# PSUM laid out anew in a two-layer graph transformer: chains, product tiles, and a standing tile for sums, weights and queries

## The chip, the cores and the metric

The kernel runs on one core of a Trainium2 chip. Its time is device time in microseconds (us) for one launch. The core has five engines that are named here as the profile names them: PE (matrix products; PEld is its loading of weights), DVE (elementwise work and reductions), ACT (activations and copies), POOL (here almost only the issuer of indirect DMAs) and SP (the issuer of plain DMAs). SBUF is the working memory of 128 partitions; PSUM is the smaller memory into which PE writes. PSUM has eight banks, each with 512 f32 per partition.

## The reference

The reference is a heterogeneous graph transformer over 6250 nodes of 128 features and 100000 edges, with 16 node types, 32 edge types, 8 heads of 16 and 2 layers.

```
k, q, v = x @ Wk[type], x @ Wq[type], x @ Wv[type]           # a matrix per node type
kw, m   = (k @ Watt[edge type])[src], (v @ Wmsg[edge type])[src]
a       = (kw * q[dst]).sum(per head) * pri[edge type] / 4
att     = softmax of a over the edges of each dst
hag     = sum over the edges of a dst of m * att
h       = silu(hag @ Wa[type]) * alpha[type] + x * (1 - alpha[type])
x       = layernorm(h) * g + b                               # twice, with weights of its own
out     = layernorm(x0 + x @ ff_w + ff_b)
```

## The kernel before

**Nodes and blocks.** A preparation sorts the nodes by type and degree into 49 blocks of 128. Forty-four blocks hold nodes of one class (four types), 11 blocks for each of four classes; five mixed blocks hold nodes of any of the 16 types. Blocks of one kind are worked on in superblocks of up to four (the mixed ones as 2 and 3).

**Tables.** A table has a row of 256 f32 for each node and edge type: the first half is the key already multiplied by Watt, the second the value multiplied by Wmsg. The table of layer 0 is made before the first edges; the table of layer 1 is made while the edges of layer 0 are worked on. Row groups are products on PE (L354 in `table_block`, a tile `tb` of two banks for each pair of products), copied to SBUF (`st`) by ACT (L362), for the last superblock in turn with DVE (L360), and written out by an indirect DMA on POOL (L1761, 98 of them, two for a block).

**Edges.** `edges(l)` walks the blocks. Each block has slots; a slot is one edge for each of its 128 nodes. For each slot POOL issues one gather (L1528, `kv<-tab,ell`, 819 in a layer) of 128 table rows. Four slots share one of 12 buffers `kv`. DVE multiplies the keys by the query (L1544), sums over each head (L1550), and when the block's slots are there, `finished` makes the softmax: maximum, difference, the exponential on ACT (its result is the weights w), the values times w, their accumulation in `acc`, and a last reduction over the four slots of `acc` into `sums`. One block (`TOP`) has additional slots whose rows are spread over its partitions; its weights stay in SBUF.

**Nodes.** `nodes` finishes a superblock: it normalises, transposes on PE, multiplies by Wa, applies silu and layernorm. In layer 0 it then makes the keys, queries and values of layer 1; in layer 1 the output. A product with a matrix per type is done by masks: for each type DVE writes `xm`, the features with every other type's columns at zero (`masked`), and PE adds up the products over the types in one PSUM tile `nb` (`linear_of`). Queries of the next superblock are made the same way (`queries0`).

**Order.** The steps of these generators are woven into the gather loop: `spread` gives a generator a number of steps over a number of slots, `tick` advances it after each chunk, `step` advances `finished`. The order on PE, DVE and ACT is then settled by a scheduler from the dependencies and the code's order; POOL's and SP's order is that of the code. Many instructions come through one helper and appear in the profile as L267.

**PSUM before**, after the preparation: one bank for `nb`, one bank `hold` for the weights of layer 0, and three tiles `tb` of two banks each, eight banks in all. In layer 0 the query is read from SBUF, where it lies; in layer 1 `query` takes a `tb` tile for each block, into which ACT copies the query (L1353), and the weights and `acc` use the same tile. In layer 0 `acc` is in SBUF.

**Mixed superblocks.** In `linear_of` the transposed features are first copied to SBUF (`h2`) when there are 16 types. For k, q, v of layer 1 the code makes three passes over the types, each with its own 16 masks:

```
for j in range(3):
    outs.append(nps.tile([P, SB * P], F32, name="nb"))
    for t0 in range(0, TY, 2):
        xms = list(masked(npl, types[t0:t0 + 2], ntb, h2, n))
```

Of the kernel before, what the change touches and what calls it, by code (L numbers as in the profile page):

```python
# [10 lines left out]
F32 = mybir.dt.float32  # L11
# [9 lines left out]
P = 128  # L21
# [51 lines left out]
def kernel(  # L73
# [240 lines left out]
    def linear_of(pool, nps, types, ntb, hT, n, w):  # L314
# [888 lines left out]
    def arm(fast):  # L1203
# [99 lines left out]
        def edges(l):  # L1303
# [43 lines left out]
            def query(s, i):  # L1347


                if l == 0:  # L1350
                    return got[s][0][:, i, :], None
                pair = tps.tile([P, 2, SB * P], F32, name="tb")
                nc.scalar.copy(pair[:, 1, :D], got[s][0][:, i, :])  # L1353
                return pair[:, 1, :D], pair

            def moved(pair, by, what, to):
# [8 lines left out]
            def finished(s, i, chunks, kvt, a, pair, sums, den):  # L1365
# [6 lines left out]
                if i0 + i == TOP:  # L1372
                    rest, chunks = kvt[-1], chunks[:-1]
                    moved(pair, node_of, rest[:, 3, :RK * REST * H],
# [13 lines left out]
                if rest is None:  # L1388
                    if l == 0:
                        held = hold_ps.tile([P, SB * P], F32, name="hold")  # L1390
                    w = (pair[:, 1, D:D + K * H] if l else held[:, :K * H]).rearrange(
                        "p (k h) -> p k h", h=H)
                on.scalar.activation(w, av, AF.Exp)
                if rest is not None:
                    moved(pair, rows_of, a[:, OWN:K, :].rearrange("p k h -> p (k h)"),
# [567 lines left out]
```

## Time and profile before

| | us |
|---|---|
| median of 3 runs (lowest to highest) | 3025.17 (3024.95 to 3028.88) |
| profiled execution | 3024.62 |
| its span | 3022.8 |
| preparation and first table | 0 to about 592 |
| gathers of layer 0, and table of layer 1 | about 592 to 1874 |
| gathers of layer 1 and output | about 1874 to 3023 |

The span is the time between the first and the last instruction of the core; the profiled execution's own time is 1.8 us longer. The first gather starts at 591.7 us, the last scatter of the table of layer 1 at 1861.4, and the first gather of layer 1 at 1874.6. Windows of 602 to 1806 and 1874 to 2977 us are used as stretches of layer 0 and layer 1.

In a row of groups, a line, an engine, an operation, and output and inputs by their names in the program are followed by the count, the busy time in us, the mean in ns, and the idle time of that engine just before these instructions with what ended it. In a row of the timeline the first two numbers are start and duration in us; in square brackets stands the idle time before and its releaser. "issue" is time in which an engine waited for nothing that the profile shows.

### The profile page before, as it was taken

How to read it: one execution, taken by the hardware profiler on the slowest of the kernel's cores; microseconds unless marked ns; L12 is line 12 of the kernel's file. 1: busy time of each engine (PE TensorE's matmuls, PEld its weight loads, DVE VectorE, ACT ScalarE, POOL GpSimd, SP SyncE). 2: the span in 40 equal slices, each digit the busy share in tenths (PEclk: the TensorE clock that was granted, in tenths of full speed). 3: DMA queues.
4: the chain of work that ended last, by engine and by line, in shares of the span. 5: the costliest groups of instructions: out<-in, count | busy, mean ns of one | idle time of the engine just before them, and what ended most of it. 6: DMA issues, size and time to landing. Idle time of an engine off the chain costs nothing.

```text
span 3022.8 us, 21562 instructions
## 1 busy us (share of the span) xinstructions
PE 1580.5 (52%) x5325; PEld 703.1 (23%) x5325; DVE 1891.1 (63%) x4383; ACT 978.7 (32%) x1635; POOL 2032.2 (67%) x2116
## 2 busy tenths in 40 slices
PE   5999978413667667777777884021122213221212
PEld 2445434201223322332223332010111001000001
DVE  7467655257657766777666653476576667666665
ACT  3887533200434234434444553011111111111111
POOL 3333665477777777777777762777677777777773
PEclk9999777556777777787777786555555556555555
DMA  7999999943677577867788897333334333333331
GB/s 217 416 418 418 394 392 397 371 107 100 234 275 260 197 248 282 297 225 254 271 303 296 330 354 278 105 110 111 92 103 118 111 111 109 112 109 106 106 100 45
DMA packets 163485, 671.37 MB, mean 222 GB/s; under 512 B 52012, under 2 KB 78926, under 8 KB 138302
## 3 DMA queue, kind: packets, MB, share of 16 engines
q0 software_dynamic: 113152, 635.19, 58.6%
q1 hardware_dynamic: 34218, 27.57, 3.3%
q10 hardware_dynamic: 15976, 7.10, 1.0%
q8 instruction: 46, 0.75, 0.1%
q14 instruction: 93, 0.76, 0.1%
HBM read 245.42 MB, written 425.02 MB: 222 GB/s over the span
## 4 chain that ended last, share of the span: by engine, by line
POOL 24%; issue 17%; DMA 16%; DVE 13%; PE 7%; ACT 3%; ACTq 0%; DVEq 0%; POOLq 0%
POOL kv L1528 21%; DMA kv<-tab,ell 14%; PE nb L267 6%; DVE kv L1544 2%; DVE xm L267 2%; PE tb L354 2%; DVE kv L267 2%; DMA tab<-st,row 2%; DVE a L1550 1%; DVE acc L267 1%; ACT L267 1%; POOL tab L1761 1%; DVE tb L267 1%; DVE hs L267 1%; POOL out_dram L1793 1%
## 5 line engine op out<-in xcount | busy, mean ns | idle before, releaser
L1528 POOL DMA_INDIRECT kv<-tab,ell x1638 | 1615.6, 986 | 542.6 <-issue 437.4
L362 ACT COPY st<-tb 128x512 f32<-128x512 f32 (+1 forms) x984 | 681.6, 777 | 535.4 <-PE tb L354 349.8
L1544 DVE TENSOR_TENSOR kv<-kv,tb 128x512 f32<-128x512 f32 (+3 forms) x223 | 142.7, 640 | 381.1 <-DMA kv<-tab,ell 367.4
L1544 DVE TENSOR_TENSOR kv<-kv,q 128x512 f32<-128x512 f32 (+3 forms) x223 | 142.9, 643 | 324.6 <-DMA kv<-tab,ell 316.1
L354 PE MATMUL tb<-bdv,vT 32*128 32x512 f32 x784 | 266.0, 781 | 45.0 <-ACT st L362 41.5
L1550 DVE TENSOR_REDUCE a<-kv 128x32 f32<-128x512 f32 (+3 forms) x446 | 280.8, 632 | 1.3
L354 PE MATMUL tb<-bdv,kvT 32*128 32x512 f32 x784 | 253.7, 790 | 22.9 <-ACT st L362 22.5
L354 PE MATMUL tb<-bdk,kvT 32*128 32x512 f32 x784 | 257.3, 776 | 7.9 <-ACT st L362 7.3
L267 PE MATMUL nb<-xm,wa 128*128 128x384 f32 (+2 forms) x336 | 178.0, 690 | 148.8 <-DVE xm L267 144.2
L267 PE MATMUL nb<-xm,wkqv 128*128 128x384 f32 (+2 forms) x504 | 218.6, 583 | 48.0 <-DVE xm L267 37.0
L1168 POOL DMA_INDIRECT tab<-st,rows x98 | 101.8, 1039 | 197.7 <-ACT st L362 169.4
L360 DVE COPY st<-tb 128x512 f32<-128x512 f32 (+1 forms) x192 | 128.7, 707 | 145.3 <-PE tb L354 74.7
L267 PE MATMUL nb<-by,all_rows 49*128 49x512 bf16 (+2 forms) x30 | 13.3, 442 | 381.6 <-DVE by L267 353.5
L354 PE MATMUL tb<-bdk,kT 32*128 32x512 f32 x784 | 210.6, 785 | 1.7 <-issue 1.6
L267 PE MATMUL nb<-ident,hag 128*128 128x128 f32 x98 | 24.6, 385 | 284.1 <-DVE hag L267 276.4
L1761 POOL DMA_INDIRECT tab<-st,row x98 | 106.1, 1083 | 80.4 <-DVE st L360 28.0
L267 PEld LDWEIGHTS nb<-xm,wkqv 128*128 128x128 f32 x504 | 106.4, 223 | 174.8 <-issue 88.6
L267 PEld LDWEIGHTS nb<-xm,wa 128*128 128x128 f32 x336 | 85.9, 272 | 240.6 <-issue 184.3
L267 DVE TENSOR_TENSOR tb<-kv,tb 128x512 f32<-128x512 f32 (+3 forms) x216 | 138.2, 640 | 0.2
L267 PE MATMUL nb<-xm,wq 128*128 128x384 f32 (+2 forms) x168 | 92.0, 708 | 87.2 <-DVE xm L267 87.1
L354 PEld LDWEIGHTS tb<-bdv,vT 32*128 32x128 f32 x784 | 98.8, 226 | 147.7 <-ACT st L362 118.9
L1353 ACT COPY tb<-hq 128x128 f32<-128x128 f32 x49 | 13.0, 267 | 369.4 <-DVE sums L267 268.8
(348 smaller groups left out, 2519.9 us busy)
## 6 DMA issues: line engine op xcount, KB each, us to landing
kv<-tab,ell POOLq DMA_INDIRECT x1638
hq<-hqx SPq DMA_DIRECT2D x7, 768.0 KB, 4.8
hqx<-hs SPq DMA_DIRECT2D x7, 512.0 KB, 3.5
hq<-hqx SPq DMA_DIRECT2D x5, 576.0 KB, 4.9
hqx<-xr SPq DMA_DIRECT2D x10, 256.0 KB, 19.2
hqx<-hs SPq DMA_DIRECT2D x5, 384.0 KB, 3.2
hr<-hqx SPq DMA_DIRECT2D x7, 256.0 KB, 5.6
tab<-st,rows POOLq DMA_INDIRECT x98
```

The source lines that it names most:

```text
L267: put = issue(*args, **kwargs)
L354: stream[nc.tensor] = nc.tensor.matmul(pt[:, b], yT[s, i * P:(i + 1) * P], bd[s, tt, :], start=True, stop=True)
L360: nc.vector.tensor_copy(to, pt)
L362: stream[nc.scalar] = nc.scalar.copy(to, pt)
L1168: put = nc.gpsimd.indirect_dma_start(out=tabs[0].rearrange("(n t) c -> n (t c)", t=16), out_offset=bass.IndirectOffsetOnAxis(ap=rows1[:, t ...
L1353: nc.scalar.copy(pair[:, 1, :D], got[s][0][:, i, :])
L1528: get = nc.gpsimd.indirect_dma_start(out=kv[:, j - j0, :], out_offset=None, in_=tabs[l][:], in_offset=bass.IndirectOffsetOnAxis(ap=ell[:, ...
L1544: stream[nc.vector] = nc.vector.tensor_tensor(kk, kk, of.unsqueeze(1).to_broadcast([P, c, D]), op=ALU.mult)
L1550: nc.vector.tensor_reduce(to, kk.rearrange("p k (h d) -> p k h d", h=H), axis=AX.X, op=ALU.add)
L1761: put = nc.gpsimd.indirect_dma_start(out=tabs[1].rearrange("(n t) c -> n (t c)", t=16), out_offset=bass.IndirectOffsetOnAxis(ap=row2[:, tg ...
L1793: put = nc.gpsimd.indirect_dma_start(out=out, out_offset=bass.IndirectOffsetOnAxis(ap=node[:, b:b + 1], axis=0), in_=o[:, i, :], in_offset ...
```

## The change

PSUM after the preparation is divided anew: two banks for `nb`, one standing tile `held` of two banks in place of `hold`, and two tiles `tb` of two banks. Bank 0 of `held` is `acc`, in both layers. The first half of bank 1 holds the weights, and the second half two places for queries that are used in turn. `query` copies the query to one of them by ACT, in layer 0 too. `moved`, which serves the additional slots of `TOP`, takes a `tb` tile in both layers.

For mixed superblocks `linear_of` no longer copies the features to SBUF; its masks read PSUM. k and v are made in one pass over the types with common masks, q in a second. Numbers of steps given to `spread` follow the removed steps.

```diff
@@ linear_of
-        if len(types) > TC:
-            h2 = pool.tile([P, SB * P], F32, name="h2", tag="hb")
-            on.scalar.copy(h2[:, :n], hT[:, :n])
-            yield
-            hT = h2
@@ arm
-        nps = ctx2.enter_context(tc.tile_pool(name="nps", bufs=1 if fast else 5, space=PSUM))
-        hold_ps = ctx2.enter_context(tc.tile_pool(name="hold", bufs=1, space=PSUM)) if fast else None
-        tps = ctx2.enter_context(tc.tile_pool(name="tps", bufs=3, space=PSUM))
+        nps = ctx2.enter_context(tc.tile_pool(name="nps", bufs=2 if fast else 5, space=PSUM))
+        turn, held = [0], None
+        if fast:
+            hold_ps = ctx2.enter_context(tc.tile_pool(name="hold", bufs=1, space=PSUM))
+            held = hold_ps.tile([P, 2, SB * P], F32, name="held")
+        tps = ctx2.enter_context(tc.tile_pool(name="tps", bufs=2 if fast else 3, space=PSUM))
@@ query, moved
-                if l == 0:
-                    return got[s][0][:, i, :], None
-                pair = tps.tile([P, 2, SB * P], F32, name="tb")
-                nc.scalar.copy(pair[:, 1, :D], got[s][0][:, i, :])
-                return pair[:, 1, :D], pair
+                at = (2 + turn[0] % 2) * D
+                turn[0] += 1
+                nc.scalar.copy(held[:, 1, at:at + D], got[s][0][:, i, :])
+                return held[:, 1, at:at + D]
-                ps = pair[:, 1, D:D + n] if pair is not None else tps.tile(
-                    [P, 2, SB * P], F32, name="tb")[:, 0, :n]
+                ps = tps.tile([P, 2, SB * P], F32, name="tb")[:, 0, :n]
@@ finished
-                    if l == 0:
-                        held = hold_ps.tile([P, SB * P], F32, name="hold")
-                    w = (pair[:, 1, D:D + K * H] if l else held[:, :K * H]).rearrange(
-                        "p (k h) -> p k h", h=H)
+                    w = held[:, 1, :K * H].rearrange("p (k h) -> p k h", h=H)
-                if rest is None and l:
-                    acc = pair[:, 0].rearrange("p (k c) -> p k c", k=CH)
-                else:
-                    acc = ep.tile([P, CH, D], F32, name="acc", bufs=1)
+                acc = held[:, 0].rearrange("p (k c) -> p k c", k=CH)
@@ steps of nodes and of queries
-                           (42 if l else 33) + (0 if len(sbs[s][2]) == TC else 14 if l else 58),
+                           (42 if l else 33) + (0 if len(sbs[s][2]) == TC else 13 if l else 41),
-                    spread(work, asked, 25 if mixed(s + 1) else 11 if l == 0 else 8, asking(s))
+                    spread(work, asked, 24 if mixed(s + 1) else 11 if l == 0 else 8, asking(s))
@@ nodes, mixed superblocks of layer 0
-                    for j in range(3):
-                        outs.append(nps.tile([P, SB * P], F32, name="nb"))
+                    for js in ((0, 1), (2,)):
+                        outs += [nps.tile([P, SB * P], F32, name="nb") for _ in js]
                         for t0 in range(0, TY, 2):
                             xms = list(masked(npl, types[t0:t0 + 2], ntb, h2, n))
                             yield
                             for t, xm in xms:
-                                on.tensor.matmul(outs[j][:, :n], wkqv[:, j, t, :], xm[:, :n],
-                                                 start=(t == 0), stop=(t == TY - 1))
+                                for j in js:
+                                    on.tensor.matmul(outs[j][:, :n], wkqv[:, j, t, :], xm[:, :n],
+                                                     start=(t == 0), stop=(t == TY - 1))
```

Over the whole of the program PE has as many instructions as before, DVE 32 fewer, ACT 43 more (49 copies of queries, less 6 of features); POOL and SP have the same instructions in the same order.

How instructions move shows at three places. The first is DVE in layer 0, where the first mixed superblock's masks (`xm`) are woven with the accumulation of the block at hand (`acc`, `hold` before). Before:

```order
L267 SCALAR_TENSOR_TENSOR xm_7726<-ntb_6465,h2_7683 128x256
L267 SCALAR_TENSOR_TENSOR xm_7728<-ntb_6465,h2_7683 128x256
L267 SCALAR_TENSOR_TENSOR xm_7735<-ntb_6465,h2_7683 128x256
L267 SCALAR_TENSOR_TENSOR xm_7737<-ntb_6465,h2_7683 128x256
L267 TENSOR_TENSOR acc_7731<-kv_7541,acc_7731 128x512
L267 SCALAR_TENSOR_TENSOR xm_7748<-ntb_6465,h2_7683 128x256
L267 SCALAR_TENSOR_TENSOR xm_7750<-ntb_6465,h2_7683 128x256
```

After:

```order
L267 SCALAR_TENSOR_TENSOR xm_7713<-ntb_6460,h2_7690 128x256
L267 TENSOR_TENSOR held_5849<-kv_7526,held_5849 128x512
L267 SCALAR_TENSOR_TENSOR xm_7722<-ntb_6460,h2_7690 128x256
L267 TENSOR_TENSOR kv_7589<-kv_7589,held_5849 128x4x128
L267 SCALAR_TENSOR_TENSOR xm_7724<-ntb_6460,h2_7690 128x256
L267 TENSOR_TENSOR held_5849<-kv_7558,held_5849 128x512
L1535 TENSOR_TENSOR kv_7740<-kv_7740,held_5849 128x4x128
```

Masks stand singly between the other instructions now, and the sums, the weights and the query all come from `held_5849`.

The second is ACT at the start of layer 0, where it makes the weights of the first blocks from the scores `a` and the queries of the next superblock. Before:

```order
L267 COPY q<-nb 128x512
L267 ACT_TABLE_LOAD
L267 ACTIVATE hold<-a 128x144
L267 ACTIVATE hold<-a 128x136
L267 ACTIVATE hold<-a 128x128
L267 CAST ntb<-nb 128x384
L267 ACTIVATE hold<-a 128x120
```

After:

```order
L267 COPY q<-nb 128x512
L267 ACT_TABLE_LOAD
L267 ACTIVATE held<-a 128x144
L1351 COPY held<-q 128x128
L267 ACTIVATE held<-a 128x136
L1351 COPY held<-q 128x128
L267 ACTIVATE held<-a 128x128
L1351 COPY held<-q 128x128
```

A copy of a query stands between each two exponentials. It writes the tile that the previous block's reduction into `sums` still reads, and waits for that reduction.

The third is PE at the joint of the layers, where the last superblock's k (`kvT0`), v (`kvT1`) and q of layer 1 and the last table products are made. Before:

```order
L267 MATMUL nb_12594<-xm_12585,wkqv_91 128x256
L354 MATMUL tb_12614<-bdk_94,kvT0_12592 128x512
L267 MATMUL nb_12601<-xm_12579,wkqv_91 128x256
L267 MATMUL nb_12601<-xm_12581,wkqv_91 128x256
L267 MATMUL nb_12601<-xm_12583,wkqv_91 128x256
L267 MATMUL nb_12601<-xm_12585,wkqv_91 128x256
L354 MATMUL tb_12614<-bdk_94,kvT0_12592 128x512
L267 MATMUL nb_12608<-ident_69,qT_12606 128x128 x2
```

After:

```order
L267 MATMUL nb_12475<-xm_12466,wkqv_91 128x256
L267 MATMUL nb_12482<-xm_12460,wkqv_91 128x256
L267 MATMUL nb_12482<-xm_12462,wkqv_91 128x256
L267 MATMUL nb_12482<-xm_12464,wkqv_91 128x256
L267 MATMUL nb_12482<-xm_12466,wkqv_91 128x256
L349 MATMUL tb_12495<-bdk_94,kvT0_12473 128x512
L267 MATMUL nb_12489<-ident_69,qT_12487 128x128 x2
L349 MATMUL tb_12495<-bdk_94,kvT0_12473 128x512
```

The first table product (L354 before, L349 now) no longer stands between v and q; both of its halves come after the products for q.

More of the change, by code (lines that the diff above doesn't have):

```diff
@@ L1373, in finished @@
                     rest, chunks = kvt[-1], chunks[:-1]
-                    moved(pair, node_of, rest[:, 3, :RK * REST * H],
+                    moved(node_of, rest[:, 3, :RK * REST * H],
                           a[:, OWN:K, :].rearrange("p k h -> p (k h)"))
@@ L1442, in finished @@
                                             op=ALU.add)
-                    moved(pair, node_of, rest[:, 2, D:], rest[:, 2, :D])
+                    moved(node_of, rest[:, 2, D:], rest[:, 2, :D])
                     yield
@@ L1492, in edges @@
             before = iter(())
-            q, pair = query(0, 0)
+            q = query(0, 0)
             for s, (i0, k, types) in enumerate(sbs):
@@ L1541, in edges @@
                         if rest:
-                            moved(pair, rows_of, got[s][0][:, i, :], kv[:, 2, :D])
+                            moved(rows_of, got[s][0][:, i, :], kv[:, 2, :D])
                         of = kv[:, 2, :D] if rest else q
@@ L1566, in edges @@
                         step(end=True)
-                    before = finished(s, i, chunks, kvt, a, pair, sums, den)
-                    q, pair = then[0] if then else (None, None)
+                    before = finished(s, i, chunks, kvt, a, sums, den)
+                    q = then[0] if then else None
             for _ in before:
```

9 lines of the change are left out of this document (5 added, 4 removed).

## The prediction

> **What bounds the kernel now.** I read the page first, then the chain of waits, then the span cut at the two layers.
>
> ```profile
> span 3022.8 us, 21562 instructions
> PE 1580.5 (52%) x5325; PEld 703.1 (23%) x5325; DVE 1891.1 (63%) x4383; ACT 978.7 (32%) x1635; POOL 2032.2 (67%) x2116
> ...
> POOL 24%; issue 17%; DMA 16%; DVE 13%; PE 7%; ACT 3%; ACTq 0%; DVEq 0%; POOLq 0%
> ...
> L1528 POOL DMA_INDIRECT kv<-tab,ell x1638 | 1615.6, 986 | 542.6 <-issue 437.4
> ```
>
> No engine is busy throughout, but the gathers of L1528 are half of the span alone, and POOL with the issue time before its instructions leads the chain. The windows by layer (columns: stretch, length, then busy time of PE, PEld, DVE, ACT, POOL, then the granted clock, DMA share, GB/s) and POOL's waits of layer 0 (total, times, longest) say how far that goes:
>
> ```profile
> 602.00:1806.00 1204.00, 832.30 (x2572) 339.52 (x2572) 799.08 (x1749) 471.52 (x639) 923.47 (x902) 0.74 0.71 251
> 1874.00:2977.00 1103.00, 210.75 (x463) 106.29 (x463) 694.10 (x1693) 146.53 (x302) 827.93 (x864) 0.54 0.37 108
> ```
> ```profile
> POOL kv L1528 <- issue: 214.2, 703, 0.3
> ...
> POOL tab L1761 <- ACT st L362: 15.1, 14, 3.5
> POOL kv L1528 <- DMA kv<-tab,ell: 11.2, 33, 1.2
> ```
>
> In layer 0 POOL is busy 923.5 us, and each of its 902 instructions has about 0.3 us of issue ahead of it (214.2/703): 923.5 + 902 x 0.305 = 1198 of 1204 us. POOL is full there. What shortens or lengthens a gather of layer 0 moves the end by that much; DVE has 1204 - 799 = 405 us to spare, ACT 732. Layer 1 adds up the same way (827.9 + 864 x 0.305 = 1091 of 1103).
>
> The same windows for the gathers alone (POOL busy and count):
>
> ```profile
> 602.00:1806.00 1204.00, 825.36 (x812) 0.74 0.71 251
> 1250.00:1430.00 180.00, 125.71 (x116) 0.79 0.69 247
> 1600.00:1800.00 200.00, 129.35 (x133) 0.74 0.88 324
> 1874.00:2977.00 1103.00, 782.08 (x819) 0.54 0.37 108
> ```
>
> The instruction is one and the same, yet takes 1016.5 ns in layer 0 (825.36/812) and 954.9 ns in layer 1 (782.08/819). It is not the DMA traffic: at 324 GB/s a gather takes 972.6 ns, at 247 GB/s 1083.7. The timeline in the first mixed superblock shows what is beside a long one:
>
> ```profile
> 1008.64 0.74 DVE L267 SCALAR_TENSOR_TENSOR xm<-ntb,h 128x256 f32<-128x256 bf16 x2
> 1008.87 2.81 POOL L1528 DMA_INDIRECT kv<-tab,ell  x1 [0.30 <-DVE sums L267]
> ...
> 1009.31 0.68 DVE L1544 TENSOR_TENSOR kv<-kv,q 128x512 f32<-128x512 f32 x1
> 1009.91 0.28 DVE L267 TENSOR_TENSOR a<-a,neg 128x128 f32<-128x128 f32 x1
> ...
> 1010.11 0.74 DVE L267 SCALAR_TENSOR_TENSOR xm<-ntb,h 128x256 f32<-128x256 bf16 x2
> ...
> 1032.09 0.95 POOL L1528 DMA_INDIRECT kv<-tab,ell  x1 [0.30 <-issue]
> 1033.34 0.95 POOL L1528 DMA_INDIRECT kv<-tab,ell  x1 [0.30 <-issue]
> ```
>
> The gather of 2.81 us runs under a train of DVE instructions that read two operands from SBUF; the two of 0.95 us run while DVE is idle. What separates the layers is just this: layer 1 keeps q, weights and sums in PSUM, layer 0 only the weights.
>
> [...]
>
> **The change, part by part.** The DVE groups of layer 0 (busy, mean ns | idle before), and the two of layer 1 that show the PSUM forms:
>
> ```profile
> L1544 DVE TENSOR_TENSOR kv<-kv,q 128x512 f32<-128x512 f32 x184 | 126.8, 689 | 298.4 <-DMA kv<-tab,ell 290.0 <-ACT q L267 7.6 <-issue 0.6
> L267 DVE TENSOR_TENSOR acc<-kv,acc 128x512 f32<-128x512 f32 x131 | 89.5, 683 | 0.0
> L267 DVE TENSOR_REDUCE sums<-acc 128x128 f32<-128x512 f32 x48 | 50.0, 1041 | 0.1
> L267 DVE SCALAR_TENSOR_TENSOR xm<-ntb,h 128x384 f32<-128x384 bf16 x80 | 41.1, 551 | 8.6 <-PE nb L267 4.0 <-ACT h L267 3.8
> L267 DVE SCALAR_TENSOR_TENSOR xm<-ntb,h 128x256 f32<-128x256 bf16 x80 | 30.1, 414 | 5.6 <-PE nb L267 5.4 <-ACT h L267 0.2
> L267 DVE SCALAR_TENSOR_TENSOR xm<-ntb,nb 128x384 f32<-128x384 bf16 x48 | 23.3, 546 | 2.5 <-PE nb L267 2.5
> ```
> ```profile
> L1544 DVE TENSOR_TENSOR kv<-kv,tb 128x512 f32<-128x512 f32 x183 | 125.5, 686 | 358.8 <-DMA kv<-tab,ell 345.1 <-issue 13.4
> L267 DVE TENSOR_REDUCE sums<-tb 128x128 f32<-128x512 f32 x46 | 31.2, 678 | 0.0
> ```
>
> 1. *Gathers.* q and the sums of layer 0 go to PSUM: kv<-kv,q and acc<-kv,acc lose their second SBUF operand. Of the 160 masks xm<-ntb,h, 96 are for k, q, v: 32 vanish, 64 stay in SBUF; the other 64 (Wq and Wa) now read PSUM. Busy time with two SBUF operands: 126.8 + 89.5 + 41.1 + 30.1 = 287.5 us before, (64/160) x 71.2 = 28.5 after, so 90% goes. The excess of layer 0's gathers is 812 x (1016.5 - 954.9) ns = 50.0 us; 90% is 45. Since the longest gather stands in a burst of masks, what stays may weigh more than its time, so I take **-42**. Bounds: -50 (all of it) and 0 (the cause is another).
>
> 2. *Scatters* share POOL and its fate (columns of the second: min, median, max ns):
>
> ```profile
> 602.00:1806.00 1204.00, 98.11 (x90) 0.74 0.71 251
> ```
> ```profile
> L1761 POOL DMA_INDIRECT tab<-st,row x98: 973/1013/3374, 779.2 to 1861.4; - x98
> ```
>
> 98.11 - 90 x 1.013 = 6.9 us over the median: **-5**, bounds -7 and 0.
>
> 3. *DVE itself.* PSUM operands are no dearer: 689 and 686 ns for the multiplication, 546 for a mask from PSUM against 551. The reduction of sums drops from 1041 to about 678 ns (48 x 0.36 = 17 us), the 32 masks are some 15 us. DVE's slack of 405 us hides all of this: 0 in the sum. If DVE had no slack it would be -32.
>
> [...]
>
> 4. *Query copies.* Layer 0 gets 49 copies of q on ACT. Layer 1 had them:
>
> ```profile
> L1353 ACT COPY tb<-hq 128x128 f32<-128x128 f32 x49 | 13.0, 267 | 369.4 <-DVE sums L267 268.8
> ```
>
> The copy must wait for the previous block's sums, since query and sums share one tile; behind it on ACT's queue stand product copies and the next exponentials, and the next block's multiplication, then its kv buffers, then POOL wait for it. In layer 1 that multiplication names no ACT wait at all, only 13.4 us of issue. In layer 0 ACT also copies products (1.01 us each, below). Bounds: 0, and 48 x (0.27 + half of 1.01) = 37 us if nothing is absorbed. Twelve kv buffers hold 48 gathers, near 60 us of POOL's time, so a lateness of 0.8 us mostly vanishes; I take **+3**, near the lower end.
>
> 5. *Two product tiles for three.* In mid-layer ACT empties them:
>
> ```profile
> PE tb L354 <- ACT st L362: 26.9, 34, 5.4
> ```
> ```profile
> ACT st L362 <- PE tb L354: 269.4, 120, 22.1
> ```
>
> ACT waits for products ten times as long as PE waits for a free tile: PE is late here, not the tiles. Nothing mid-layer; bounds 0 and the price in rival two. The joint between the layers is another matter, there nothing gathers:
>
> ```profile
> 1841.41 1.12 PE L354 MATMUL tb<-bdk,kvT 32*128 32x512 f32 x2
> ...
> 1847.01 2.36 DVE L360 COPY st<-tb 128x1024 f32<-128x1024 f32 x2 [12.41 <-PE tb L354]
> ...
> 1853.03 1.19 PE L354 MATMUL tb<-bdv,kvT 32*128 32x512 f32 x8 [0.25 <-DVE st L360]
> ...
> 1854.20 1.01 ACT L362 COPY st<-tb 128x1024 f32<-128x1024 f32 x1 [1.17 <-PE tb L354]
> ...
> 1859.43 1.23 DVE L360 COPY st<-tb 128x1024 f32<-128x1024 f32 x1 [0.99 <-PE tb L354]
> ...
> 1861.41 0.97 POOL L1761 DMA_INDIRECT tab<-st,row  x1 [4.17 <-issue]
> ...
> 1874.62 0.99 POOL L1528 DMA_INDIRECT kv<-tab,ell  x1 [12.24 <-DMA tab<-st,row]
> ```
>
> The last superblock's 16 products are emptied from 1847.01 to 1860.66, 13.65 us, by ACT and DVE in turn. With two tiles a pair is filled (1.19) and then emptied (1.23): 1.23 + 7 x 2.42 = 18.2, or +4.5. Against it, k, v and q follow on PE without a table matmul of 1.12 us between them and with a bank more for chains, about -1.4; the sums are 0.36 shorter twice, -0.7; leftover products of the superblock before now compete for two tiles, about +1.5. I take **+4**, bounds 0 and +10.
>
> 6. *Layer 1* already had this layout; its sums move to another tile: 0.
>
> Sum: -42 - 5 + 3 + 4 = -40. The profiled execution is 3024.62 us, 1.8 of it around the span; 3024.62 - 40 = 2984.6. The median of the runs is 0.55 above the profiled one, so **2985 us**.
>
> **The rivals.**
>
> *The gathers stay long.* If what lengthens them is something else that layer 0 does (products, scatters), terms 1 and 2 are gone and 3 and 4 stay: 3024.6 + 7 + 0.55 = 3032. For it: the cause is read from neighbours in time alone. Against it: the pair of rows at 1008.87 and 1032.09.
>
> *Two product tiles become the bound of layer 0.* This is the case on the other side. The scatters stand in POOL's order between the gathers; a late product stops the gathers behind it, which the 15.1 us of tab<-ACT st already show. 98 scatters take four tiles each (two for keys, two for values), 196 pairs; if each pair lost half a fill, 0.3 us (from 1.19/2 for one tile), that is 59 us: 3025.2 - 47 + 7 + 59 = 3044. It decides from 40 us on, that is 0.41 us per scatter. For it: the clock there is 0.74 and PE the busiest engine after POOL (832 of 1204). Against: ACT's 269.4 us of waiting for products.
>
> *The query copies come late.* Half of term 4's upper bound or more reaches POOL: 3025.2 - 47 + 4 + (18 to 37) = 3000 to 3019, the middle 3010.
>
> *All of it comes.* -50 and -7 in full, joint and copies at 0, and DVE being lighter ends some of the small waits: 2957 to 2967.
>
> **How the numbers follow.** Main case 0.68, query copies 0.10, all of it 0.12, gathers stay 0.05, two tiles bind 0.05. A measurement of this kernel can tell about 0.2%, 6 us, from no change: faster is below 3019, slower above 3031. Faster: 0.68 + 0.12 + nearly all of 0.10 = 0.89. Same: 0.01 of the late copies and 0.03 of the first rival, 0.04. Slower: 0.05 + 0.02 = 0.07. The main case alone spans about 2972 to 2998 (joint and copies at their ends, gathers at -50 to -35). The range, 2962 to 3014, takes in most of the copies' case and half of the full gain and leaves out about 0.17.
>
> **What would show it.** Right: a mean of the gathers of layer 0 of 0.965 us or less (1.0165 now), with the stretch from the first gather to the last scatter some 45 us shorter; POOL still full there; DVE's masks from nb 64 more. The joint from the last product's matmul to the first gather of layer 1 some 4 us longer. Layer 1 unchanged within 5 us. Wrong: gathers still over 1.0 us (the cause), tab<-ACT st over 40 us (the tiles), or an idle of POOL put down to kv buffers with ACT held<-q before it (the copies).

## The result and the profile after

The changed kernel takes 2977.36 us (median of 4 runs, 2976.48 to 2982.34), the kernel before 3025.06 us beside it (3022.4 to 3028.88): ratio 0.9842, 95% interval 0.9828 to 0.9855. Forecast were 2985 us, 2962 to 3014.

The page of the changed kernel:

```profile
span 2976.3 us, 21675 instructions
PE 1670.6 (56%) x5325; PEld 727.2 (24%) x5325; DVE 1895.5 (64%) x4351; ACT 996.6 (33%) x1678; POOL 1975.7 (66%) x2116
...
L1519 POOL DMA_INDIRECT kv<-tab,ell x1638 | 1566.8, 957 | 531.6 <-issue 422.5
```

The gathers (L1519 now) are 48.8 us shorter in all. The windows of the gathers' line, of layer 0 and of layer 1 (stretch, length, POOL's busy time and count, granted clock, DMA share, GB/s), before:

```profile
591.00:1802.00 1211.00, 833.48 (x819) 0.74 0.71 250
1874.00:2977.00 1103.00, 782.08 (x819) 0.54 0.37 108
```

and after:

```profile
593.00:1760.00 1167.00, 786.56 (x819) 0.71 0.74 260
1844.00:2935.00 1091.00, 780.27 (x819) 0.54 0.37 109
```

Layer 0's gathers fell from 1.0177 to 0.9604 us each while more DMA traffic ran beside them (260 GB/s, 250 before). To see where the rest of the time went, the span is cut at the first and last gather of each layer. POOL's timeline at the joint of the layers, before (the rest of it stands in the prediction):

```profile
1801.03 0.97 POOL L1528 DMA_INDIRECT kv<-tab,ell  x1 [0.31 <-DVE acc L267]
...
1822.68 0.97 POOL L1761 DMA_INDIRECT tab<-st,row  x1 [4.68 <-ACT st L362]
1850.11 0.97 POOL L1761 DMA_INDIRECT tab<-st,row  x1 [26.46 <-DVE st L360]
```

and after:

```profile
1758.09 0.98 POOL L1519 DMA_INDIRECT kv<-tab,ell  x1 [0.30 <-DVE held L267]
1764.54 1.01 POOL L1753 DMA_INDIRECT tab<-st,row  x1 [5.47 <-ACT qT L267]
...
1788.63 0.97 POOL L1753 DMA_INDIRECT tab<-st,row  x1 [5.45 <-ACT st L357]
1814.95 0.97 POOL L1753 DMA_INDIRECT tab<-st,row  x1 [25.35 <-DVE st L355]
...
1835.53 0.97 POOL L1753 DMA_INDIRECT tab<-st,row  x1 [5.89 <-issue]
1844.87 0.99 POOL L1519 DMA_INDIRECT kv<-tab,ell  x1 [8.37 <-DMA tab<-st,row]
```

| stretch, us | before | after | difference |
|---|---|---|---|
| to the first gather | 591.7 | 593.8 | +2.0 |
| layer 0, first to last gather | 1210.3 | 1165.3 | -44.9 |
| joint, to the first gather of layer 1 | 72.6 | 85.8 | +13.2 |
| layer 1, first to last gather | 1101.8 | 1090.0 | -11.8 |
| after the last gather | 46.4 | 41.5 | -4.9 |
| span | 3022.8 | 2976.3 | -46.5 |

So layer 0 gave what was forecast, the joint lost three times as much, and layer 1 with what follows its last gather, forecast at nothing, gave 16.7 us. The layer 0 row is made of -46.9 us of gathers, -5.7 us of scatters and +7.6 us of gaps between POOL's instructions.

The +13.2 us of the joint have four parts. Nine scatters stand there in both kernels, five with products left over from the superblock before the last and four of the last one. From the last gather to the fifth scatter it took 30.5 us, 21.6 before (+8.9); from there to the first of the last four 26.3, 27.4 before (-1.1); the last four span 20.6, 11.3 before (+9.3); and from the last scatter to the first gather of layer 1 it took 9.3, 13.2 before (-3.9).

In the last four scatters' stretch ACT and DVE copy the products in turn. Four rows of that after:

```profile
1815.78 1.01 ACT L357 COPY st<-tb 128x1024 f32<-128x1024 f32 x1 [2.20 <-PE tb L349]
1816.40 1.23 DVE L355 COPY st<-tb 128x1024 f32<-128x1024 f32 x1 [2.20 <-PE tb L349]
...
1818.97 1.01 ACT L357 COPY st<-tb 128x1024 f32<-128x1024 f32 x1 [2.17 <-PE tb L349]
1819.83 1.23 DVE L355 COPY st<-tb 128x1024 f32<-128x1024 f32 x1 [2.20 <-PE tb L349]
```

Each copy is as long as before (1.01 and 1.23 us), but each waits 2.2 us for its tile to be filled; a pair takes 3.43 us, not 2.4. PE's granted clock in that stretch (length, PE's busy time, clock) was 1.00 before and 0.51 after:

```profile
1845.00:1859.00 14.00, 11.70 (x64) 1.00 0.58 243
```
```profile
1810.00:1834.00 24.00, 21.91 (x57) 0.51 0.60 250
1836.00:1846.00 10.00, 0.00 (x0) 0.50 0.96 370
```

Layer 1: the 11 us are one stall, at the block with additional slots (`TOP`). Its 28 slots hold eight of the twelve buffers until its softmax is done. Before, DVE began that softmax (`a<-a,neg` of 336 columns) when 227 gathers of layer 1 were out and the buffers full, and POOL waited:

```profile
2173.59 0.50 DVE L267 TENSOR_TENSOR a<-a,neg 128x336 f32<-128x336 f32 x1
...
2181.30 1.22 POOL L1528 DMA_INDIRECT kv<-tab,ell  x1 [11.29 <-DVE t L267]
```

After, DVE began it when 222 were out; it stood earlier in DVE's order, behind 58 of layer 1's multiplications with the query and not behind 61, ahead of some that wait for later gathers:

```profile
2134.09 0.50 DVE L267 TENSOR_TENSOR a<-a,neg 128x336 f32<-128x336 f32 x1
...
2142.19 0.94 POOL L1519 DMA_INDIRECT kv<-tab,ell  x1 [1.52 <-DVE held L267]
```

### The profile page after: what moved, and what is told of

It reads as the page before. It is cut to its first block, busy times and chain, and to the rows that moved or that the text cites. A ratio compares the mean times of both kernels' runs of the same rounds, so it can differ in the third digit from the quotient of the medians.

```text
span 2976.3 us, 21675 instructions
## 1 busy us (share of the span) xinstructions
PE 1670.6 (56%) x5325; PEld 727.2 (24%) x5325; DVE 1895.5 (64%) x4351; ACT 996.6 (33%) x1678; POOL 1975.7 (66%) x2116
## 5 line engine op out<-in xcount | busy, mean ns | idle before, releaser
L1519 POOL DMA_INDIRECT kv<-tab,ell x1638 | 1566.8, 957 | 531.6 <-issue 422.5
L1535 DVE TENSOR_TENSOR kv<-kv,held 128x512 f32<-128x512 f32 (+3 forms) x446 | 284.9, 640 | 549.7 <-DMA kv<-tab,ell 459.5
L349 PE MATMUL tb<-bdk,kvT 32*128 32x512 f32 x784 | 295.9, 888 | 45.9 <-ACT st L357 45.7
L349 PE MATMUL tb<-bdv,kvT 32*128 32x512 f32 x784 | 286.3, 898 | 42.0 <-ACT st L357 41.6
L267 DVE TENSOR_TENSOR held<-kv,held 128x512 f32<-128x512 f32 (+3 forms) x444 | 287.2, 647 | 8.7
L349 PE MATMUL tb<-bdv,vT 32*128 32x512 f32 x784 | 261.8, 789 | 50.6 <-ACT st L357 46.5
L267 PE MATMUL nb<-xm,wa 128*128 128x384 f32 (+2 forms) x336 | 185.7, 716 | 88.7 <-DVE xm L267 84.8
L267 PE MATMUL nb<-xm,wkqv 128*128 128x384 f32 (+2 forms) x504 | 205.5, 562 | 10.2 <-DVE xm L267 10.2
L267 DVE TENSOR_TENSOR kv<-kv,held 128x512 f32<-128x512 f32 (+3 forms) x336 | 208.9, 622 | 2.2
L349 PE MATMUL tb<-bdk,kT 32*128 32x512 f32 x784 | 207.6, 790 | 2.4 <-issue 1.6
L267 DVE SCALAR_TENSOR_TENSOR xm<-ntb,nb 128x512 f32<-128x512 bf16 (+2 forms) x304 | 157.3, 562 | 32.3 <-PE nb L267 30.1
L1753 POOL DMA_INDIRECT tab<-st,row x98 | 100.0, 1020 | 103.2 <-DVE st L355 37.1
L267 ACT ACTIVATE held<-a 128x128 f32<-128x128 f32 (+7 forms) x96 | 27.5, 287 | 325.9 <-DVE a L267 182.4
L267 PEld LDWEIGHTS nb<-xm,wkqv 128*128 128x128 f32 x504 | 104.5, 216 | 121.7 <-issue 46.9
L349 PEld LDWEIGHTS tb<-bdv,vT 32*128 32x128 f32 x784 | 97.1, 228 | 148.4 <-ACT st L357 118.4
```

The source lines that it names most:

```text
L267: put = issue(*args, **kwargs)
L349: stream[nc.tensor] = nc.tensor.matmul(pt[:, b], yT[s, i * P:(i + 1) * P], bd[s, tt, :], start=True, stop=True)
L1519: get = nc.gpsimd.indirect_dma_start(out=kv[:, j - j0, :], out_offset=None, in_=tabs[l][:], in_offset=bass.IndirectOffsetOnAxis(ap=ell[:, ...
L1535: stream[nc.vector] = nc.vector.tensor_tensor(kk, kk, of.unsqueeze(1).to_broadcast([P, c, D]), op=ALU.mult)
L1753: put = nc.gpsimd.indirect_dma_start(out=tabs[1].rearrange("(n t) c -> n (t c)", t=16), out_offset=bass.IndirectOffsetOnAxis(ap=row2[:, tg ...
```

## The experiments

Each run's profile was cut into the same stretches. "Changed" is the changed kernel; times are medians, with the ratio to the kernel before and its 95% interval; a profile shows one execution. How far executions differ by themselves can be read from kernels in which a layer is written alike. The gathers of layer 0 add up to 786.5 to 788.2 us in the five kernels that have the changed layer 0, those of layer 1 to 780.3 to 783.5 us in the seven that have the changed layer 1. The gaps between POOL's instructions in layer 0 come to 283.9 to 291.9 us in the former, and their layer 0 to 1162.2 to 1169.0 us.

**Does a second SBUF operand lengthen the gathers?** Three runs each put one operand of the changed kernel back into SBUF.

```diff
# the query of layer 0 (of layer 1 in the third run)
+                if l == 0:
+                    return got[s][0][:, i, :]
                 at = (2 + turn[0] % 2) * D
# acc of layer 0
+                if l == 0:
+                    acc = ep.tile([P, CH, D], F32, name="acc", bufs=1)
```

> The changed kernel, but layer 0 reads its query from SBUF again, without the 49 copies; all else stays. Theory (a DVE instruction with two SBUF operands lengthens the gather beside it): the 143 us of kv<-kv,q in layer 0 have two SBUF operands again. Before, 320 us of such instructions went with 50 us of excess, 0.156 us per us: the gathers of layer 0 grow by 22 us, their mean from 0.960 to about 0.987 us, and the time from 2977 to 2992 to 3002 us. Rival A (only the masks lengthen gathers): mean stays at 0.960, time 2975 to 2980. Rival B (the query copies cost time): the time falls below 2975.

Measured 2999.08 us (0.9908, 0.9891 to 0.9924). Layer 0 is 25.2 us longer, of which gathers 16.7 us and scatters 2:

```profile
593.00:1785.00 1192.00, 803.31 (x819) 0.70 0.73 255
```

> The changed kernel, but acc of layer 0 is a tile in SBUF again; all else stays. Theory of the two SBUF operands: 106 us of acc<-kv,acc at 0.156 us per us make 16 us, the mean of the gathers of layer 0 goes from 0.960 to about 0.980 us, the time to 2988 to 2998 us. Rival A (only the masks): 2977 to 2980 us, the mean stays.

Measured 2988.32 us (0.987, 0.9853 to 0.9886), at the lower end of the expected range: the median is 11 us above the changed kernel's, the profiled execution 16. Gathers were 19.1 us longer:

```profile
595.00:1779.00 1184.00, 805.68 (x819) 0.71 0.73 256
```

> The changed kernel, but layer 1, where no table is made and PE and ACT are nearly idle, reads its query from SBUF; layer 0 stays as changed. The original kernel had the query of layer 1 in PSUM too, so this makes the contention anew where it never was. Theory of the two SBUF operands: about 141 us of the multiplication in layer 1 at 0.156 make 22 us; the mean of the gathers of layer 1 goes from 0.953 to about 0.98 us and the time to 2992 to 3002 us; layer 0 stays at 0.960. Rival C (the long gathers belong to the work on tables in layer 0, its products and scatters): layer 1 stays at 0.953 and the time at 2977.

Measured 3001.74 us (0.992, 0.9903 to 0.9936), in the expected range but for another reason. Layer 1's gathers grew by 7.0 us only, and layer 0's stayed:

```profile
591.00:1759.00 1168.00, 787.18 (x819) 0.70 0.74 260
1844.00:2953.00 1109.00, 787.35 (x819) 0.54 0.37 107
```

The rest is the stall at `TOP`, back with 11.7 us, and the end after the last gather, back at 47.3 us. So the query and the sums carry 36 of layer 0's 47 us, but the price of 0.156 us per us of DVE work did not hold: 0.117 for the query and 0.18 for the sums in layer 0, and 0.05 at most in layer 1, where 3 of the 7 us are within what executions differ by.

That three effects of like size stood in one total called for a run that changes the memory and leaves the waits alone.

```diff
-            held = hold_ps.tile([P, 2, SB * P], F32, name="held")
+            held = npl.tile([P, SB * P + 200 + D], F32, name="held")
-                at = (2 + turn[0] % 2) * D
+                at = SB * P + 200
-            ntb = npl.tile([P, SB * P], BF16, name="ntb", bufs=4)
+            ntb = npl.tile([P, SB * P], BF16, name="ntb", bufs=3)
```

> The changed kernel with the standing tile in SBUF in place of PSUM: sums, weights and query stay one tile, written and waited for by the same instructions, but all its readers on DVE have two SBUF operands. For its room the query has one place, not two, and the types of a superblock have three buffers, not four. Measured so far: undoing the query alone in layer 0 added 16.7 us to the gathers (0.117 us per us of such DVE work), the sums alone 19.1 us, the query alone in layer 1 only 7.0 us (0.05). Theory (the place in memory lengthens the gathers): in layer 0 query, weights and sums together are about 380 us of DVE work, so gathers grow by 44 to 69 us, to a mean of 1.015 to 1.045 us; in layer 1 by 20 to 45 us, to 0.977 to 1.007 us. The stall of 11 us at the block with additional slots and the end after the last gather (46 or 41 us): if the wait of the query's copy for the whole standing tile is what put these right in the changed kernel, they stay away here, since the waits are the same; time 3041 to 3091 us. If the place in memory did it, they come back, 16 us more. Rival (only the order of instructions changed the gathers): means stay near 0.960 and 0.953, time 2977 to 2985 us.

With one place for the query, the last multiplications of a block read the query of the next block, so the scores are computed with a wrong query in part; the instructions and their shapes are the same. Measured 3119.29 us (1.0317, 1.0299 to 1.0334):

```profile
590.00:1819.00 1229.00, 852.41 (x819) 0.72 0.70 247
1899.00:3066.00 1167.00, 849.17 (x819) 0.54 0.35 102
```

Gathers are 65.8 us longer in layer 0 (within the expected 44 to 69) and 68.9 us longer in layer 1 (expected 20 to 45). Layer 1 has no table work, moves 102 GB/s and its PE is busy for 213 of 1167 us, and yet its gathers take 1.037 us as layer 0's take 1.041: products, scatters and traffic of layer 0 are not the cause. The memory of DVE's operands is. The stall at `TOP` was 6.4 us, between the two expectations; the end stayed at 40.4 us.

**The masks.** Two runs: the last masks with two SBUF operands moved to PSUM, and the whole part on mixed superblocks undone (one bank for chains, features copied to SBUF, three passes).

```diff
# masks of k, q, v from PSUM
-                    h2 = npl.tile([P, SB * P], F32, name="h2", tag="hb")
-                    on.scalar.copy(h2[:, :n], hT[:, :n])
+                    h2 = hT
-                    for js in ((0, 1), (2,)):
+                    for js in ((0,), (1,), (2,)):
```

> The changed kernel, but the masks for k, q, v of mixed superblocks read the features from PSUM, as those for Wa do, in three passes (32 masks more, one copy per superblock less). Theory: the last 28.5 us of masks with two SBUF operands go; at 0.117 to 0.156 us per us that is 3 to 4.5 us, more if masks weigh more, as the prediction held: mean of the gathers of layer 0 from 0.960 to 0.953 to 0.956 us, time 2970 to 2974 us. Rival: the 32 masks more and the bank held over all passes make nodes late in mixed superblocks; an idle of POOL appears and the time is above 2980 us.

Measured 2979.44 us (0.9851, 0.9835 to 0.9868). The gathers took 0.9567 us each, 3.1 us less in all, near what was expected; the time did not move (layer 0 was 1165.1 us long, as in the changed kernel). Layers 0 that are written alike differ by 7 us from one execution to another, so 3 us cannot be found again there.

```diff
# part on mixed superblocks undone
-bufs=2 if fast else 5, space=PSUM
+bufs=1 if fast else 5, space=PSUM
+        if len(types) > TC:
+            h2 = pool.tile([P, SB * P], F32, name="h2", tag="hb")
+            on.scalar.copy(h2[:, :n], hT[:, :n])
-                    for js in ((0, 1), (2,)):
+                    for js in ((0,), (1,), (2,)):
```

> The changed kernel without its part on mixed superblocks and chains: one bank for chains, features copied to SBUF in front of the masks, three passes for k, q, v. Standing tile and two product tiles stay (one bank idle). By the prediction's terms: 43 us of masks with two SBUF operands are back, 5 to 7 us of gathers, and at the joint k, q, v wait for their copies again, 1.4 us: 2983 to 2987 us. Rival (the second bank for chains is what made layer 1 and the end of the kernel shorter, as its nodes ran in chains there): layer 1's stall and the end come back with 16 us, 2995 to 3003 us.

Measured 3003.14 us (0.9934, 0.9917 to 0.995), 26 us above the changed kernel, its profiled execution 17 us above. The time is at the upper edge of the rival's range, but not for the rival's reason: the stall did not come back and the end was 43.1 us. The gathers of layer 0 took 5.0 us more, as the masks' 43 us should, and its scatters and gaps 6 more; the joint was 2 us longer, layer 1 and the end 4 and 1.6. The 4 us of layer 1 are gathers, not gaps (784.7 us against 780.3; its 32 masks for mixed superblocks read SBUF again, and part of it may be chance). The other 9 us of the median this one trace does not show. So the second bank may be worth more than its masks, but no single wait was found for it.

**What ended the stall in layer 1?** First suspect was the small products for `TOP`, which shared a tile with the query.

```diff
-                ps = pair[:, 1, D:D + n] if pair is not None else tps.tile(
-                    [P, 2, SB * P], F32, name="tb")[:, 0, :n]
+                ps = tps.tile([P, 2, SB * P], F32, name="tb")[:, 0, :n]
```

> The original kernel, but the three small products for the block with additional slots take a product tile of their own in layer 1 too, as in the changed kernel. Theory M (they waited on the tile that they shared with the query): the stall of 11.3 us in layer 1 goes, time 3013 to 3017 us. Theory W (the stall is a matter of the order on DVE, which the query copy's wait in the changed kernel shifts): the stall stays, 10 to 12 us, and the time is 3021 to 3029 us.

Measured 3026.65 us (1.0003, 0.9993 to 1.0013), the stall 11.4 us: it was not the products' tile. Next, the query's copy out of the standing tile, in the kernel with one bank for chains, which leaves a bank free:

```diff
+            own_q = hold_ps.tile([P, SB * P], F32, name="own_q")
-                nc.scalar.copy(held[:, 1, at:at + D], got[s][0][:, i, :])
-                return held[:, 1, at:at + D]
+                nc.scalar.copy(own_q[:, at:at + D], got[s][0][:, i, :])
+                return own_q[:, at:at + D]
```

> The kernel without the part on mixed superblocks and chains (3003 us), and the query copies go to a bank of their own, so that they wait for no reduction any more; memory of all operands stays PSUM. Theory W: without that wait the stall of 10 to 12 us in layer 1 comes back, and 3 to 5 us at the end; in layer 0 POOL's gaps grow by about 6 us, as they did when the copies were left out; gathers keep their mean of 0.967 and 0.958. Time 3017 to 3026 us. Rival (the place in memory or the number of tiles did it): 3000 to 3006 us.

Measured 3020.46 us (0.9987, 0.9977 to 0.9997), against 3003.14 with the query in the standing tile. All operands are in PSUM as before, and POOL's timeline has the stall again; the end is 47.0 us, 4 us longer:

```profile
2166.40 1.21 POOL L1525 DMA_INDIRECT kv<-tab,ell  x1 [11.35 <-DVE t L267]
```

In all kernels here in which sums, weights and layer 1's query share one standing tile in PSUM, the stall is away; in the two in which that query lies elsewhere (in SBUF, in a bank of its own) it is back with 11.7 and 11.4 us. What changed is the order in which DVE is given its work. In every trace without the stall the softmax of `TOP` comes behind 58 of layer 1's multiplications, with 222 gathers out; in every trace with 11 us of stall behind 61, with 227 out; with the standing tile in SBUF, 6.4 us, behind 60, with 226 out. The last pair of kernels differs in the query's tile alone, so the query's place in the standing tile set this order. That it did so because the copy has to wait for the readers of that tile is argued, not shown: the scheduler goes by dependencies, and these are what the place changes. Which of those readers would matter is open, as the next run shows.

**Two product tiles.** The change of three tiles to two alone, on the original kernel:

```diff
-        tps = ctx2.enter_context(tc.tile_pool(name="tps", bufs=3, space=PSUM))
+        tps = ctx2.enter_context(tc.tile_pool(name="tps", bufs=2 if fast else 3, space=PSUM))
```

> The original kernel with two product tiles in place of three and nothing else changed. In layer 1, where the query, the weights and the sums of a block take one of these tiles, the copy of the next query must now wait for the block before it, as in the changed kernel. Theory: layer 0 between the gathers keeps its length within 5 us (rival two of the prediction: 40 to 59 us longer); the joint grows by 10 to 14 us, with the granted clock near 0.51 in its last stretch; and by theory W (the query copy's wait changes the order on DVE) the stall of 11 us in layer 1 and 5 us of the end go. Time 3018 to 3026 us. Without theory W: 3033 to 3041 us.

Measured 3049.16 us (1.0073, 1.0057 to 1.009), 24 us slower and above both expected ranges. Layer 0 grew by 6.7 us, not 40 to 59; the joint by 14.5; layer 1 by 3.6, and the stall stayed (11.3 us), so a wait for the block before alone does not move DVE's order. This refutes that form of theory W: the copy in the changed kernel also waits for the multiplications of the block at hand, which read the same tile, and that may be what matters.

At the joint the standing tile is idle. It can be the third product tile for the last superblock:

```diff
+        class Three:
+            def tile(self, *args, **kwargs):
+                third[0] += 1
+                return held if third[0] % 3 == 0 else tps.tile(*args, **kwargs)
-                yield from steps(table_block(ep, tps, kT, vT, i, share, STB, store,
+                yield from steps(table_block(ep, Three() if share else tps, kT, vT, i, share, STB, store,
```

> The changed kernel, but the products of the last superblock take the standing tile, idle at the joint, as a third product tile in turn. Theory (at the joint filling and emptying take turns since there are two tiles): a pair took 2.2 us of filling plus 1.23 us of emptying, 3.43 us; with three tiles it takes what PE needs, 2.2 to 2.4 us, so eight pairs end 7 to 9 us earlier and the time is 2968 to 2971 us. Rival D (PE at its granted clock of 0.50 is the limit): less than 2 us, 2975 to 2979 us.

Measured 2968.9 us (0.9803, 0.9781 to 0.9824), the lowest median here and in the range of the theory. But its four runs lie in two groups, at 2963 to 2964 and at 2974 to 2975 us, and the median falls between them; the profiled execution is one of the longer. In it the last four scatters span 11.3 us, not 20.6, as in the kernel before; the way from the last scatter to the first gather is 3.6 us longer again, so the joint is 6.5 us shorter. The clock is 1.00 again:

```profile
1811.00:1826.00 15.00, 12.21 (x63) 1.00 0.63 262
```

Is the low clock the cause or a companion? A run kept PE busy with two tiles:

```diff
+                    for _ in range(2 if warm is not None else 0):
+                        stream[nc.tensor] = nc.tensor.matmul(
+                            warm[:, :2 * P], ident, kT[:, :2 * P], start=True, stop=True)
```

> The changed kernel with its two product tiles, but at the joint PE makes two further products of 128x256 after each tile, into a bank that nothing reads; the wanted work is the same. With two tiles PE's granted clock in the last stretch of the joint was 0.51 in each of the kernels run so far, with three tiles 1.00. Theory K (waiting between fills lets the clock drop, and the low clock doubles the fills): with PE kept busy the clock is above 0.8 there, a pair takes 1.14 + 1.23 = 2.4 us as the prediction had it, the last four scatters span 12 to 15 us in place of 20.6, and the time is 2967 to 2973 us. Rival (the clock is low there for another reason): the further products of 0.93 us per tile come on top of fills at 0.51, four scatters span over 22 us, time 2979 to 2987 us.

Measured 2983.71 us (0.9863, 0.9845 to 0.9881). The clock rose to 1.00, as theory K said:

```profile
1806.00:1834.00 28.00, 28.00 (x108) 1.00 0.55 214
```

But the time went up. The further products took 1.06 us per tile, not half of that as I had reckoned, so PE, busy for all of the 28 us, spent 2.12 us on each tile and was itself the limit (four scatters in 25.4 us). What the run shows is that a tile was filled in 1.06 us at a clock of 1.00, where the changed kernel takes 2.2, and that with the further products PE was granted 1.00 in this stretch, 0.51 without them. What two tiles would take there at the full clock, 1.06 + 1.23 = 2.3 us a pair, was not seen.

Two tiles at the full clock can be seen earlier in the joint, where ACT alone empties the products left over from the superblock before. The changed kernel, and the kernel whose query has a bank of its own:

```profile
1770.00:1789.00 19.00, 18.49 (x48) 0.50 0.85 359
```
```profile
1782.00:1800.00 18.00, 16.14 (x63) 1.00 0.93 391
```

Scatters are 6.4 us apart in the first and 4.5 us in the second. A scatter needs four tiles, so two fills and two copies one after the other: 2 x (2.2 + 1.01) = 6.4 us, or, with the fill of 1.13 us that the second trace shows, 2 x (1.13 + 1.01) = 4.3 us. Both kernels have two tiles, so two tiles do not by themselves bring the low clock. What brought it in one and not in the other is open.

One more attempt let DVE help with the superblock before the last as well:

```diff
-                table(pieces_of(i0, k, outs[0], outs[1], (2,) if final else ()))
+                table(pieces_of(i0, k, outs[0], outs[1], (2,) if fast and i0 in (sbs[-1][0], sbs[-2][0]) else ()))
```

> The kernel with the standing tile as third product tile at the joint (2969 us), and DVE also copies half of the products of the superblock before the last, whose last five scatters come after the last gather of layer 0, 5.4 us apart. Theory (ACT alone empties them there): they come 3.5 to 4.5 us apart, time 2960 to 2966 us. Rival (DVE's copies delay the last block's softmax, or PE at its clock of 0.6 is what is late): 2966 to 2973 us.

Measured 2976.75 us (0.9837, 0.982 to 0.9853), 8 us above the median without it and above both expected ranges: the five scatters came 6.8 to 7.1 us from start to start, 6.1 to 6.4 without it (the 5.4 us of the expectation is the idle time between them). The clock there was 0.67 (0.63 without it), and ACT's copies had not been what was late. The fills at the low clock are the larger part of each turn, and a turn with DVE's copy is longer, 2.2 + 1.23 = 3.43 us against 2.2 + 1.01; two turns make a scatter's 6.9 us.

## Why the prediction was right, and where it was not

**Term 1, the gathers (-42 forecast): right.** -46.9 us. Taking the parts back one by one gave 16.7 (query), 19.1 (sums) and 5.0 us (masks and chains), 41 of the 47; the other 6 no run took back. The bursts of masks, which the prediction held to weigh more, show no sign of it: 3.1 us for the last 28.5 us of them, 5.0 for 43, 0.11 to 0.12 us per us, each figure known to some 2 us.

**Term 2, the scatters (-5): right.** In layer 0 their mean fell from 98.11/90 = 1.090 us to 1.024:

```profile
604.00:1756.00 1152.00, 90.11 (x88) 0.71 0.74 260
```

**Term 3, DVE (0): right.** The groups of layer 0 after show no dearer operand in PSUM (684 against 689 ns, 692 against 683), and sums at 686 ns against 1041:

```profile
L1535 DVE TENSOR_TENSOR kv<-kv,held 128x512 f32<-128x512 f32 x181 | 123.8, 684 | 188.9 <-DMA kv<-tab,ell 133.2 <-ACT held L1351 51.9 <-ACT st L357 2.2
...
L267 DVE TENSOR_TENSOR held<-kv,held 128x512 f32<-128x512 f32 x172 | 119.1, 692 | 3.3
...
L267 DVE TENSOR_REDUCE sums<-held 128x128 f32<-128x512 f32 x47 | 32.2, 686 | 0.7
```

**Term 4, the query copies (+3): the mechanism was mis-seen.** The first row above shows that the copies did come late: the multiplication waited 51.9 us for them, more than the upper bound of 37. The wait for data of gathers fell from 290.0 to 133.2 us at the same time, so it was mostly time in which DVE would have waited anyway. And leaving the copies out did not shorten layer 0's gaps (293.7 us, 287.6 with them, 6 us that are not clear of the 8 by which executions differ). The buffers absorbed the late copies, as far as POOL goes, and the rival fell with that. The 7.6 us of gaps belong for the larger part to the next term.

**Term 5, two tiles.** Nothing mid-layer: nearly right. PE waits for tiles three times as long (26.9 us before):

```profile
PE tb L349 <- ACT st L357: 83.0, 90, 7.7
```

The rival on the other side needed this lateness at the scatters. Most of it stayed on PE, but not all. POOL's waits for product copies between the first and the last gather of layer 0 (total, times, longest), before and after:

```profile
POOL tab L1761 <- ACT st L362: 5.4, 11, 2.1
```
```profile
POOL tab L1753 <- ACT st L357: 9.8, 13, 5.5
```

With two tiles alone they came to 16.4 us, and layer 0 grew by 6.7 us, far from the 40 that the rival needed.

The joint, +4 forecast with bounds 0 and +10, came to +13.2. The step that failed is the fill of 1.19 us, taken from rows at a clock of 1.00 and used for a stretch that was then granted 0.51. The serial form, fill and then empty, was right: 2.2 + 1.23 = 3.43 us a pair, and the last four scatters cost +9.3 us where +4.5 was reckoned. The second term that was too small is that of the leftover products, put at about +1.5: they cost +8.9. Of these, +5.2 lie between the five scatters and have the same reason, since fill and copy by ACT take turns there as well, at a clock of 0.50 (24.0 us against 18.9 before, and 18.6 with two tiles at the full clock); +3.7 are a later first scatter. Against these stand -1.1 in place of -2.1 for k, v, q and the sums, and -3.9 that the sum did not have: the first gather of layer 1 came sooner behind the last scatter (12.24 us of waiting before, 8.37 after, 11.94 with the third tile). Why, no run shows.

**Term 6, layer 1 (0): wrong by 16.7 us.** The argument was that layer 1 had the layout already. It had the memory (but for 32 masks of 15 us in all), not the order: with the query in the standing tile DVE gets another order, and the stall of 11 us, which the profile of before showed, goes. With it go some 5 us at the end, for which the runs show no cause of its own; the end was 46 to 47 us in every kernel with the stall of 11 us and 40 to 43 in the others. It was not in the sum; the case "all of it comes" named small waits but not this one.

Joint +9 and layer 1 -17 against the forecast, gaps +7.6 in place of +3, gathers and scatters 6 further down and 2 us more before the first gather: together the profiled execution came 6.5 us below its forecast, and the median 8. The sign and most of the size rest on terms 1 and 2, which the runs bear out; that the total came this near owes something to misses that cancel.

**The rivals.** That the gathers stay long is excluded by their mean of 0.960 us, and that something else in layer 0 lengthens them by the run with the standing tile in SBUF: there a gather of layer 0 took 1.041 us, 0.960 with the tile in PSUM, and layer 1 as a whole was 76 us longer. Tensor_tensor instructions are what got a second SBUF input in that run.

## What to carry to other kernels

Where POOL issues DMAs back to back, look at what stands beside its long instructions: here moving one DVE operand of each pair to PSUM shortened the mean gather of layer 0 by nearly 6% (1.0177 to 0.9604 us) at no price for DVE (689 ns for the multiplication before, 684 after). Price a stage by the clock that it will have after the change (0.51 in the last stretch of the joint here), not by the one that the trace of before shows (1.00). And when operands come to share a tile, list the new waits and look where the order moves, in stages that keep their layout too.

## What the runs showed of the hardware

In the last stretch of the joint PE's granted clock changed with the number of tiles and of products: it was 1.00 before and with the third tile, 0.50 to 0.59 in all kernels with two tiles and nothing else for PE to do, and 1.00 with two tiles and further products. It was 0.50 in the 10 us of the changed kernel without any product. The busy share that the profile shows did not tell which it would be: PE was busy for 11.70 of 14 us at 1.00 before, and for 21.91 of 24 us at 0.51 after, where a fill took 2.2 us (1.06 at 1.00 with the further products). And two tiles ran at 1.00 for 18 us in one kernel and at 0.50 for 19 us in another, at the same kind of work.

The reduction over a strided 128x512 operand took 1041 ns from SBUF and 686 ns from PSUM, while in layer 0 multiplications (689 ns with the query in SBUF, 684 in PSUM), additions (683 and 692 ns) and masks of 384 columns (551 and 546 ns) cost nearly the same from both.

How much a DVE instruction with two SBUF operands lengthens a gather beside it was not constant (0.05 to 0.18 us per us; the lowest rests on 7 us, of which 3 may be chance). It may depend on when in the gather it falls; that was not tried.
